# Layer 0's attention: scores once with queries on partitions, exp per half of the keys, turned by TensorE, against scores computed twice

## The chip, the core and the metric

The kernel runs on one core of one Trainium2 chip. The metric is device time of one execution in microseconds (us), the median over runs. A core has five engines that work at the same time and hand work to each other with semaphores: TensorE (PE; the loading of its stationary operand is listed apart, as PEld), VectorE (DVE), ScalarE (ACT), GpSimd (POOL) and SyncE (SP, which issues transfers). Each engine executes its own queue in order.

## The reference, cut to what matters

Two pre-norm transformer layers over `x` of 2 x 1024 x 128, in float32. Layer 0's attention has 8 heads; per head the queries and keys are 128 + 32 wide and come from a 32-wide latent:

```
scores = einsum('bhsd,bhtd->bhst', q, k) / sqrt(160)
attn   = softmax(scores, axis=-1)
o      = einsum('bhst,bhtd->bhsd', attn, v_c)
x      = x + concat(o) @ W_O + b_O
```

After it come a mixture of experts (8 experts, 2 per token, and a shared one), layer 1's causal attention (16 heads of 8) and layer 1's expert layer. The change touches layer 0's attention alone.

## The kernel before, in words

Products of weights are folded ahead, so that a head's score is a product over 64 numbers (32 latent and 32 rotary ones): `q2` holds two heads, one on partitions 0 to 63 and one on 64 to 127, and `key2` holds the keys twice. Two score matmuls of one pair of heads therefore sit on different row groups of the array. A batch and four heads make a unit `i` of 0 to 3; a unit is two pairs of heads (`pr`).

**Scores are computed twice.** `maxima0` (L562) computes them with queries on partitions: per 128 queries, 512 keys and pair of heads two matmuls into a two-bank PSUM tile `sc` (L574), and VectorE takes the negated maximum along the keys (L578). Every four query tiles the maxima are combined (L590), rounded by GpSimd into three bfloat16 parts (L593 to L601), and turned into rows by 16 small matmuls (`rows`, L603) that ScalarE copies out (L614). `attend0` (L618) computes the scores again with keys on partitions (L640), adds the negated maximum of each query with a bfloat16 matmul against ones (L646), and one ScalarE exp handles 128 keys x 2 heads x 512 queries (L651). The exps then already have the keys on partitions, so four column-tiled matmuls of 32 columns (`values`, L676) multiply them by the values, summed over the 8 key tiles in the PSUM tile `ud`. The denominators come from sums of the exps over key tiles (GpSimd, in the last unit VectorE, L662), closed by matmuls with ones (L693). `end` (L686) queues the rest: reciprocals of 128 x 128 tiles on VectorE (L706), the product (L709), a projection by `w_vo` (L714) and an add to `x` (L718).

PSUM has 8 banks: `ps` three tiles of two banks, `pn` and `pu` one each.

**What sets the order.** Instructions are issued in the order in which the program makes them on PE, DVE, POOL and SP (`IN_ORDER`, L44); ScalarE's are placed by the scheduler. The passes are generators that advance in turns (L831): one step of `maxima0`, one of `attend0` that starts `LAG` = 23 steps later (L736), one of `more`, which brings queries of the next unit (L544) and the preparation of batch 1 (L491). In the last steps (L838) the routing of batch 0 (`route`, L224) and the gathers of its rows (`get`, L386) are put beside. What is left of `late` runs among the first expert blocks (`quotients`, L988). All these end with unit 3; the expert blocks (L891) follow on PE.

Of the kernel before, what the change touches and what calls it, by code (L numbers as in the profile page):

```python
# [29 lines left out]
DA = DC + 1  # L30
QSCALE = 1.0 / math.sqrt(128 + DR)
# [20 lines left out]
def two_layers(ctx: ExitStack, tc: tile.TileContext, a: dict, out: bass.AP):  # L52
# [166 lines left out]
    w_vo = u_pool.tile([P, 2, D], F32, name="w_vo", bufs=1)  # L219
# [181 lines left out]
    with ExitStack() as att:  # L401

        ps = att.enter_context(tc.tile_pool(name="ps", bufs=3, space=PSUM))
# [5 lines left out]
        e0_pool = att.enter_context(tc.tile_pool(name="e0", bufs=10))  # L409
        s_pool = att.enter_context(tc.tile_pool(name="s", bufs=4))  # L410

        def bank0():
            return ps.tile([P, 512], F32, tag="ps", name="bank0")

        def spare0():
            t = e0_pool.tile([P, 2, 512], F32, tag="ex0", name="spare")
            return t.rearrange("p a b -> p (a b)")

        quot_bank = [lambda: pn.tile([P, 512], F32, tag="pn", name="y")]
# [3 lines left out]
        w_lat = load("w_lat", [P, 160], a["w_lat"])  # L423
        b_q = load("b_q", [DC, 1], a["b_q"])
# [5 lines left out]

        g = wa.tile([DA, H0, DC + DR], F32, name="g")
        nc.scalar.dma_start(g[:, :, DC : DC + DR], a["w_qr"])
# [22 lines left out]
        ctx_b, qs, last_rows = {}, {}, {}  # L455

        def products():
            gp = ps.tile([P, H0, DA], F32, tag="ps", name="gp")
            for h in range(H0):
                nc.tensor.matmul(  # L460
                    gp[:DA, h, :], w_up[:, 0, h, :], w_up[:, 1, h, :], start=True, stop=True
                )
            nc.vector.tensor_copy(g[:, :, 0:DC], gp[:DA, :, 0:DC])
            nc.vector.tensor_scalar(gc, gp[:DA, :, DC], QSCALE, None, ALU.mult)

        def output():


            vo = ps.tile([P, 2, D], F32, tag="ps", name="vo")
            for hg in range(2):  # L470
                for j in range(4):
                    h = 4 * hg + j
                    nc.tensor.matmul(
                        vo[DC * j : DC * (j + 1), hg, :], w_up[:, 2, h, 0:DC], w_o[:, h, :],
                        start=True, stop=True,
                    )
# [14 lines left out]
        def prepare(b):  # L491

            xt = xt_pool.tile([P, S], F32, name="xt")
            xn = e0_pool.tile([P, NT, D], F32, tag="ex0", name="xn0")
            yield from layernorm_steps(b, bank0, xt, xn, fine=b > 0, pool=b > 0, wait=4, by=nc.gpsimd if b else nc.vector)
            cq = lat.tile([DA, S], F32, name="cq")
            nc.gpsimd.memset(cq[DC:DA, :], 1.0)
# [3 lines left out]
            pk = ps.tile([P, S], F32, tag="ps", name="pk")  # L501
            for i in range(2):
                cols = slice(512 * i, 512 * (i + 1))
                nc.tensor.matmul(
                    pq[:DC, cols], w_lat[:, 0:DC], xt[:, cols], start=True, stop=True
                )
            for i in range(2):
# [4 lines left out]
            nc.vector.tensor_scalar(cq[0:DC, :], pq[:DC, :], b_q, None, ALU.add)  # L512
# [6 lines left out]
            pv = ps.tile([P, NT, DC], F32, tag="ps", name="pv")  # L519
# [9 lines left out]
            pc = ps.tile([P, NT, H0], F32, tag="ps", name="pc")  # L529
            for n in range(NT):  # L530
                nc.tensor.matmul(
                    pc[:, n, :], cq[:, n * P : (n + 1) * P], gc, start=True, stop=True
                )
            nc.vector.tensor_copy(cc.rearrange("p h n -> p n h"), pc)
            yield
# [8 lines left out]
        def queries(i):  # L544

            b, hg = divmod(i, 2)
            cq = ctx_b[b][0]
            qs[i] = []
            for pr in range(2):
                pq = ps.tile([P, S], F32, tag="ps", name="pq")  # L550
                h = 4 * hg + 2 * pr
                for c in range(2):
                    cols = slice(512 * c, 512 * (c + 1))
                    nc.tensor.matmul(  # L554
                        pq[:, cols], g[:, h : h + 2, :], cq[:, cols], start=True, stop=True
                    )
                q2 = q_pool.tile([P, S], F32, tag="q2", name="q2")
                nc.scalar.activation(q2, pq, AF.Copy, scale=QSCALE)
                qs[i].append(q2)
                yield  # L560

        def maxima0(i):  # L562

            b, hg = divmod(i, 2)
            _, key2, _, cc = ctx_b[b]
            mx2 = small.tile([P, 4, NT, 2], F32, name="mx2a", bufs=2)
            rows = None
            for st in range(NT):
                for c in range(2):
                    for pr in range(2):  # L570
                        sc = ps.tile([P, 2, 512], F32, tag="ps", name="sc")
                        for j in range(2):
                            r = slice(64 * j, 64 * (j + 1))
                            nc.tensor.matmul(  # L574
                                sc[:, j, :], qs[i][pr][r, st * P : (st + 1) * P],
                                key2[r, 512 * c : 512 * (c + 1)], start=True, stop=True,
                            )
                        nc.vector.tensor_reduce(  # L578
                            mx2[:, 2 * pr : 2 * pr + 2, st, c], sc, AX.X, ALU.max,
                            negate=True,  # L580
                        )
                        yield
                    if rows and c:
                        rows()
                        rows = None
                if st % 4 == 3:
                    half = st // 4
                    sts = slice(4 * half, 4 * half + 4)
                    m4 = small.tile([P, 4, 4], F32, name="m4", bufs=2)
                    nc.vector.tensor_reduce(m4, mx2[:, :, sts, :], AX.X, ALU.min)  # L590

                    ch = cc[:, 4 * hg : 4 * hg + 4, sts]
                    nc.gpsimd.tensor_tensor(m4, m4, ch, ALU.subtract)  # L593
                    nc.gpsimd.tensor_tensor(m4, m4, ch, ALU.add)
                    mp = mps[half]
                    for k in range(3):
                        nc.gpsimd.tensor_copy(mp[:, :, :, k], m4)
                        if k < 2:
                            r = small.tile([P, 4, 4], F32, name=f"mq{k}", bufs=2)
                            nc.gpsimd.tensor_tensor(r, m4, mp[:, :, :, k], ALU.subtract)  # L600
                            m4 = r  # L601

                    def rows(half=half, mp=mp):  # L603
                        pm = ps.tile([P, 2, 512], F32, tag="ps", name="pm")
                        for j in range(4):
                            for n in range(4):
# [8 lines left out]

            last_rows[i] = rows

        def attend0(i):  # L618


            b, hg = divmod(i, 2)
# [938 lines left out]
```

## Time and profile before

| | |
|---|---|
| median of 9 runs | 946.29 us (940.41 to 952.91) |
| profiled execution | 948.51 us, of which the span is 946.8 us |
| first score matmul (L574) | 22.0 us from the span's start |
| last values matmul (L676) of layer 0 ends | about 421 us |
| first expert block's turned rows (L902) | 424.1 us |
| PE, DVE, ACT, POOL busy over the span | 92%, 60%, 44%, 44% |
| mean granted TensorE clock | 0.971 |

Times below are microseconds from the span's start. In groups, a line is: source line, engine, operation, output <- input, shapes, count, busy time and mean duration. In timelines it is: start, length from the first start to the last end of merged instructions, engine, line, operation, count, and in brackets the idle time before and what ended it. A float32 matmul is recorded as two instructions, a float32 transpose (a matmul against the identity) as one. PE records overlap, since matmuls are pipelined; the time a matmul takes of the queue is read from start to start, and when its result is ready from its end.

### The profile page before, as it was taken

The page shows a single profiled execution, that of the slowest core. Times are in us where ns is not written, and L with a number is a line of the kernel's source. Part 1 is how long each engine was busy: PE and PEld are TensorE (multiplying, and loading weights), DVE is VectorE, ACT ScalarE, POOL GpSimd, SP SyncE. Part 2 cuts the span into 40 slices and gives each one's busy share as a digit, 9 for nine tenths or more (in the row PEclk, how much of TensorE's full clock was granted, in tenths as well). Part 3 has the DMA queues.
Part 4 walks back from the last instruction along what each step waited for, and adds up shares of the span by engine and source line. Part 5 has one row for each costly group of instructions (what it writes and reads, how often), then busy time and mean ns, then how long its engine had stood idle before and what let it go on. Part 6 is the DMA issues. An engine that isn't in the chain of part 4 may idle for free.

```text
span 946.8 us, 14370 instructions
## 1 busy us (share of the span) xinstructions
PE 867.1 (92%) x5308; PEld 426.9 (45%) x5308; DVE 572.1 (60%) x999; ACT 416.9 (44%) x685; POOL 413.4 (44%) x572
## 2 busy tenths in 40 slices
PE   5899999999999999999899789888889999889986
PEld 2543334443333333437675457553334444544334
DVE  4765553536464569756632484776787767666613
ACT  1024433443334343454322144245467665666672
POOL 3018794756584941356046320018432432313521
PEclk9799999999999999999989999988899999999999
DMA  9100000000000000013212126014233123020000
GB/s 284 32 1 1 1 1 1 1 1 1 1 1 2 1 17 7 9 28 103 31 52 45 19 64 144 31 42 71 33 70 70 37 41 52 2 63 15 19 1 23
DMA packets 32825, 33.48 MB, mean 35 GB/s; under 512 B 5548, under 2 KB 30028, under 8 KB 31596
## 3 DMA queue, kind: packets, MB, share of 16 engines
q1 hardware_dynamic: 26882, 25.02, 11.3%
q0 software_dynamic: 4544, 5.91, 3.6%
q10 hardware_dynamic: 1331, 1.65, 0.5%
q8 instruction: 43, 0.70, 0.3%
q14 instruction: 25, 0.20, 0.1%
HBM read 24.10 MB, written 8.45 MB: 34 GB/s over the span
## 4 chain that ended last, share of the span: by engine, by line
PE 70%; DVE 14%; ACT 4%; issue 4%; DMA 4%; POOL 3%; SPq 0%; POOLq 0%; ACTq 0%; DVEq 0%
PE sc L574 12%; PE sc L640 11%; PE ud L676 6%; PE up L1298 6%; PE banks L1155 4%; DVE mx L1165 4%; PE gub L917 4%; PE bank L1273 4%; ACT ex L1278 3%; PE sc L646 3%; DVE mx2a L578 2%; PE yblk L945 2%; PE gu L871 2%; PE den L693 1%; PE pq L554 1%
## 5 line engine op out<-in xcount | busy, mean ns | idle before, releaser
L578 DVE TENSOR_REDUCE mx2a<-sc 128x2 f32<-128x1024 f32 x128 | 154.6, 1217 | 131.8 <-PE sc L574 131.7
L651 ACT ACTIVATE ex<-sc 128x1024 f32<-128x1024 f32 x128 | 131.1, 1024 | 196.9 <-PE sc L646 192.3
L1165 DVE TENSOR_REDUCE mx<-banks 128x2 f32<-128x1024 f32 (+3 forms) x160 | 174.6, 1113 | 65.3 <-PE banks L1160 54.9
L1278 ACT ACTIVATE ex<-bank 128x512 f32<-128x512 f32 (+2 forms) x320 | 157.8, 558 | 101.0 <-PE bank L1273 97.5
L574 PE MATMUL sc<-key,q 64*128 64x512 f32 x512 | 148.6, 633 | 1.7 <-DVE mx2a L578 1.7
L662 POOL TENSOR_TENSOR sum<-sum,ex 128x1024 f32<-128x1024 f32 x60 | 139.7, 2353 | 8.8 <-ACT ex L651 8.7
L640 PE MATMUL sc<-q,key 64*128 64x512 f32 x512 | 140.6, 602 | 0.4 <-DVE probs L242 0.4
L1282 POOL TENSOR_SCALAR_AFFINE_SELECT ex<-ex 128x128 f32<-128x128 f32 (+1 forms) x192 | 66.8, 371 | 133.7 <-ACT ex L1278 129.9
L1155 PE MATMUL banks<-kp,qp 72*128 72x512 bf16 (+3 forms) x384 | 100.8, 335 | 6.0 <-DVE mx L1165 4.2
L1273 PE MATMUL bank<-qp,kp 75*128 75x512 bf16 (+3 forms) x384 | 96.2, 333 | 9.1 <-ACT ex L1278 6.1
L393 POOL DMA_INDIRECT xb<-xn,row x46 | 53.1, 1154 | 93.6 <-PE bank L902 35.3
L1298 PE MATMUL up<-ex,vp 128*32 128x512 f32 (+3 forms) x768 | 80.3, 514 | 3.6 <-POOL ex L1282 3.6
L574 PEld LDWEIGHTS sc<-key,q 64*128 64x128 f32 x512 | 49.3, 189 | 64.7 <-issue 51.2
L640 PEld LDWEIGHTS sc<-q,key 64*128 64x128 f32 x512 | 51.1, 188 | 60.6 <-issue 43.3
L978 POOL DMA_INDIRECT got<-ys,pos x32 | 41.3, 1291 | 77.3 <-DMA ys<-yb 64.0
L917 PE MATMUL gub<-wall,xbt 128*128 x184 | 65.1, 478 | 8.3 <-DVE mx L1165 6.2
L676 PE MATMUL ud<-ex,val 128*32 128x512 f32 x512 | 68.3, 604 | 0.0
L1155 PEld LDWEIGHTS <-qp 72*128 72x128 bf16 x384 | 37.8, 100 | 50.6 <-issue 34.2
L662 POOL TENSOR_TENSOR sum<-ex,ex 128x1024 f32<-128x1024 f32 x12 | 28.0, 2354 | 71.4 <-ACT ex L651 71.4
L922 ACT ACTIVATE slb<-gub 128x352 f32<-128x352 f32 x46 | 21.4, 464 | 77.1 <-PE gub L917 77.0
L923 DVE TENSOR_TENSOR hds<-slb,gub 128x352 f32<-128x352 f32 x46 | 23.7, 515 | 50.2 <-ACT slb L922 50.2
L646 PE MATMUL sc<-mr,onesb 64*128 64x512 bf16 x256 | 53.2, 378 | 0.0
(267 smaller groups left out, 1084.3 us busy)
## 6 DMA issues: line engine op xcount, KB each, us to landing
qp<-parts SPq DMA_DIRECT2D x72, 64.0 KB
kp<-parts SPq DMA_DIRECT2D x72, 64.0 KB
parts<-qk SPq DMA_DIRECT2D x24, 128.0 KB
ys<-yb SPq DMA_DIRECT2D x10, 256.0 KB
wall<-in_ffn_gate_dram SPq DMA_DIRECT2D x1, 1584.0 KB
wall<-in_ffn_up_dram SPq DMA_DIRECT2D x1, 1584.0 KB
wall<-in_ffn_down_dram SPq DMA_DIRECT2D x2, 576.0 KB
x<-in_h_dram SPq DMA_DIRECT2D x4, 256.0 KB
```

What stands on the lines that cost most here:

```text
L574: nc.tensor.matmul(sc[:, j, :], qs[i][pr][r, st * P : (st + 1) * P], key2[r, 512 * c : 512 * (c + 1)], start=True, stop=True,)
L578: nc.vector.tensor_reduce(mx2[:, 2 * pr : 2 * pr + 2, st, c], sc, AX.X, ALU.max, negate=True,)
L640: nc.tensor.matmul(sc[:, j, :], key2[r, k * P : (k + 1) * P], qs[i][pr][r, cols], start=True, stop=False,)
L651: nc.scalar.activation(ex, sc, AF.Exp)
L662: adder.tensor_tensor(t, a1, ex, ALU.add)
L676: nc.tensor.matmul(ud[DC * j : DC * (j + 1), :], val[:, k, :], es[j // 2][:, j % 2, :], start=(k == 0), stop=(k == NT - 1),)
L917: nc.tensor.matmul(gu[:, s, 0:FF], xbts[j // 4][:, (j % 4) * P : (j % 4 + 1) * P], flat[:, bass.ds(e0 + FF * s, FF)], start=True, stop=True,)
L1155: nc.tensor.matmul(sc[:, n, 0:w], qp[0:KP, j, s0 : s0 + P], kp[0:KP, j, c0:c1], start=True, stop=not diag,)
L1165: nc.vector.tensor_reduce(to, sc[:, :, 0:w], AX.X, ALU.max, negate=True)
L1273: nc.tensor.matmul(sc[:, j, 0:w], kp[0 : KP + 3, j0 + j, t0 : t0 + P], qp[0 : KP + 3, j0 + j, lo:hi], start=True, stop=True,)
L1278: nc.scalar.activation(ex[:, :, 0:w], sc[:, :, 0:w], AF.Exp, scale=SCALE1)
L1298: nc.tensor.matmul(up[WH * j : WH * (j + 1), lo - c0 :], vps[b][:, k, h : h + WH], es[j], start=(k == 0), stop=end,)
```

## The change

Layer 0's scores are computed once, with queries on partitions. A block is 256 queries (`QT` = 2 tiles) of one pair of heads, 32 blocks in all; per block four tiles of 128 queries x 512 keys x 2 heads (`scores`). VectorE takes the negated maximum over this half of the keys, two small VectorE operations pass it through a rounding by `cc`, and ScalarE applies exp per head with the maximum as per-partition bias and the sum as accumulated output (`accum_out`). TensorE then turns the exps in 128 x 128 pieces (`weights`, four steps `k` of two banks with four transposes each); the banks are copied to SBUF by ScalarE, every fourth copy by VectorE (`evict`). `values` multiplies them by the values, with the two halves of the keys of each head on partition groups of their own, in `uds`. At a block's end small tensors give the factor of each half, exp(common minimum - own) / denominator (`scale_a` to `scale_c`); it is widened by GpSimd to 128 columns, turned by TensorE and copied by ScalarE (`scale_d`), multiplied in (`times`) and projected (`add`; `w_vo` holds each head's product twice).

PSUM is now: `ps` two tiles of two banks (scores), `pt` two banks (`turned`, shared by the exps' transposes, `scale_d` and the projection's result), `pn` and `pu` one each. ScalarE's order is the program's too (`ALL_IN_ORDER`). Steps of `weights` run four steps behind `scores`. The latent queries are kept on two row groups (`CQ`), so that the two halves of a query matmul run on different rows; `queries` makes one pair of heads per four blocks. The routing of batch 0 and its gathers are put beside batch 1's blocks. The work removed is: the second scores, the bfloat16 matmuls, the rows, the sums on GpSimd, the denominators' matmuls, and the wide reciprocals.

The diff, cut to its core:

```diff
-        ps = att.enter_context(tc.tile_pool(name="ps", bufs=3, space=PSUM))
+        ps = att.enter_context(tc.tile_pool(name="ps", bufs=2, space=PSUM))
+        pt = att.enter_context(tc.tile_pool(name="pt", bufs=2, space=PSUM))
...
+        def turned():
+            return pt.tile([P, 512], F32, tag="pt", name="turned")
+
+        quot_bank = [turned]
...
+        def scores(n):
+            b, pr, c = BLOCKS[n]
...
+            for t in range(QT):
+                st = QT * c + t
+                for m in range(2):
+                    flush0()
+                    sc = ps.tile([P, 2, 512], F32, tag="ps", name="sc")
+                    for j in range(2):
+                        r = slice(64 * j, 64 * (j + 1))
+                        nc.tensor.matmul(
+                            sc[:, j, :], q2[r, st * P : (st + 1) * P],
+                            key2[r, 512 * m : 512 * (m + 1)], start=True, stop=True,
+                        )
+                    lo = low[:, t, m, :]
+                    nc.vector.tensor_reduce(lo, sc, AX.X, ALU.max, negate=True)
+                    ch = cc[:, 2 * pr : 2 * pr + 2, st]
+                    nc.vector.tensor_tensor(lo, lo, ch, ALU.subtract)
+                    nc.vector.tensor_tensor(lo, lo, ch, ALU.add)
+                    ex = e0_pool.tile([P, 2, 512], F32, name="ex0")
+                    exps[n][2][t, m] = ex
+                    def last(t=t, m=m, sc=sc, ex=ex):
+                        for j in range(2):
+                            nc.scalar.activation(
+                                ex[:, j, :], sc[:, j, :], AF.Exp, bias=low[:, t, m, j : j + 1],
+                                accum_out=tot[:, t, m, j : j + 1],
+                            )
+                    due0.append(last)
+                    yield
...
+        def evict(to, src):
+            copies[0] += 1
+            if copies[0] % 4:
+                nc.scalar.copy(to, src)
+            else:
+                nc.vector.tensor_copy(to, src)
+
+        def weights(n):
...
+            def scale_a():
+                both = small0("both", True)
+                nc.vector.tensor_tensor(both, low[:, :, 0, :], low[:, :, 1, :], ALU.min)
+                by = small0("by")
+                nc.vector.tensor_tensor(
+                    by, both.unsqueeze(2).to_broadcast(shape), low, ALU.subtract
+                )
+                nc.scalar.activation(by, by, AF.Exp)
+                by_block["by"] = by
+            def scale_b():
...
+                nc.gpsimd.tensor_tensor(tot, tot, by, ALU.mult)
+                den = small0("den", True)
+                nc.gpsimd.tensor_tensor(den, tot[:, :, 0, :], tot[:, :, 1, :], ALU.add)
+            def scale_c():
...
+                nc.vector.reciprocal(den, den)
+                nc.gpsimd.tensor_tensor(
+                    by, by, den.unsqueeze(2).to_broadcast(shape), ALU.mult
+                )
+                wide = u_pool.tile([P, QT, 4, DC], F32, name="wide")
+                nc.gpsimd.tensor_copy(
+                    wide,
+                    by.rearrange("p t m j -> p t (m j)").unsqueeze(3).to_broadcast([P, QT, 4, DC]),
+                )
+            def scale_d():
+                tp = turned()
+                for t in range(QT):
+                    nc.tensor.transpose(
+                        tp[:, t * P : (t + 1) * P],
+                        by_block["wide"][:, t].rearrange("p k r -> p (k r)"), ident,
+                    )
+                by_t = u_pool.tile([P, W], F32, name="by_t")
+                nc.scalar.copy(by_t, tp[:, 0:W])
...
+            def times():
+                ot = u_pool.tile([P, W], F32, name="ot0")
+                nc.vector.tensor_tensor(ot, ud, by_block["t"], ALU.mult)
...
+            def add():
+                y = quot_bank[0]()[:, 0:W].rearrange("p (n d) -> p n d", d=D)
+                for t in range(QT):
                     nc.tensor.matmul(
+                        y[:, t, :], by_block["ot"][:, t * P : (t + 1) * P], w_vo[:, pr, :],
+                        start=True, stop=True,
                     )
+                n0 = b * NT + QT * c
+                nc.vector.tensor_add(x[:, n0 : n0 + QT, :], y, x[:, n0 : n0 + QT, :])
+
+            mine = [scale_a, scale_b, scale_c, scale_d, times, add]
+            for k in range(4):
                 if late:
                     late.pop(0)()
+                if ended and k < 3:
+                    ended.pop(0)()
+                es = []
+                for m in range(2):
+                    tp = turned()
+                    for j in range(2):
+                        for t in range(QT):
+                            i = QT * j + t
+                            nc.tensor.transpose(
+                                tp[:, i * P : (i + 1) * P],
+                                ex[t, m][:, j, k * P : (k + 1) * P], ident,
+                            )
+                    e = et_pool.tile([P, 2, W], F32, name="et")
+                    evict(e.rearrange("p j w -> p (j w)"), tp)
+                    es.append(e)
+                def values(k=k, es=es):
+                    for m in range(2):
                         for j in range(2):
+                            r = 64 * m + DC * j
                             nc.tensor.matmul(
+                                ud[r : r + DC, :], val[:, 4 * m + k, :], es[m][:, j, :],
+                                start=(k == 0), stop=(k == 3),
                             )
+                late.append(values)
+                if k:
+                    mine.pop(0)()
+                yield
+            ended.extend(mine)
...
         passes = zip_longest(
-            chain(*map(maxima0, range(n))), after(LAG, chain(*map(attend0, range(n)))), more()
+            chain(*map(scores, range(n)), once(flush0)),
+            after(2 * QT, chain(*map(weights, range(n)))),
+            more(),
         )
-        with tc.manual_schedule(engines=IN_ORDER):
-            for _ in islice(passes, (n - 1) * UNIT + LAG - 2):
+        with tc.manual_schedule(engines=ALL_IN_ORDER):
+            for _ in islice(passes, QT * n + 2 * QT + 4):
                 pass
-            ahead = chain(hurry(route(0, bank0, spare0), 2), get(0))
+            ahead = chain(hurry(spread(route(0, bank0, spare0), 2), 3), get(0))
             for _ in passes:
                 next(ahead, None)
```

## The prediction, on record before the result

> **What bounds the kernel now.** I read the page's busy shares first, then its costliest groups, then a table of stages, then a timeline of PE. Layer 0's attention takes 22 to 421 us, 399 of the span's 946.8 us. In the table of stages (columns: time, then busy time of PE, PEld, DVE, ACT and POOL, then the granted clock) PE is busy almost without a gap where both passes run, and no other engine is above 65%:
>
> ```profile
> 22.00:65.00 43.00, 39.14 (x188) 21.44 (x186) 28.90 (x30) 3.06 (x3) 3.90 (x8) 0.84 0.15 28
> 65.00:370.00 305.00, 304.10 (x1774) 119.83 (x1772) 168.19 (x198) 122.93 (x126) 199.09 (x142) 1.00 0.01 3
> 370.00:421.00 51.00, 49.70 (x321) 19.45 (x319) 39.93 (x73) 26.37 (x27) 24.06 (x22) 0.97 0.06 16
> ```
>
> Busy is no proof of a peak, so I take starts from the PE timeline (start, length):
>
> ```profile
> 215.76 1.02 PE L574 MATMUL sc<-key,q 64*128 64x512 f32 x4
> 216.62 1.02 PE L640 MATMUL sc<-q,key 64*128 64x512 f32 x4
> 217.47 0.38 PE L646 MATMUL sc<-mr,onesb 64*128 64x512 bf16 x2
> ...
> 219.72 1.06 PE L676 MATMUL ud<-ex,val 128*32 128x512 f32 x8
> 220.72 1.13 PE L574 MATMUL sc<-key,q 64*128 64x512 f32 x4
> ```
>
> A score pair holds PE for 0.86 us (215.76 to 216.62), 0.96 after another form of matmul; the ones 0.22 or 0.31 (219.41 to 219.72); four values matmuls 1.00. So PE's queue is the bound, and the stage is worth what its queue holds, until another engine or a wait is later.
>
> **PE's work, old and new.** Old: 128 score pairs x 0.96 = 123; 128 second pairs with their ones x 1.1 = 141; 64 values x 1.0 = 64; denominators 8 x 1.75 = 14; projections 8 x 1.1 = 9; rows 8 x 0.6 = 5; 8 query tiles x 1.75 = 14; batch 0's leftovers (folded weights, value and bias products between 24 and 50 us) 12, batch 1's preparation 10, routing 8. Sum 400 against 399 seen: nothing is left to waits.
>
> New: 128 score pairs stay (123). 1024 transposes come in. Their price stands in the expert blocks:
>
> ```profile
> 452.75 0.47 PEld L902 LDWEIGHTS bank<-ident,xb 128*128 128x128 f32 x4
> 452.86 0.60 PE L902 MATMUL bank<-ident,xb 128*128 128x128 f32 x4
> 453.19 0.89 PEld L917 LDWEIGHTS gub<-wall,xbt 128*128 128x128 f32 x4
> ```
>
> Four take from 452.75 to 453.19: 0.11 us each, though one record lasts 0.27. With 0.1 for the change of form, eight cost 0.98 per score pair: 125. Values have the same columns in matmuls of 256: half of 1.0 per pair, plus up to 0.1: 68 to 80. The factors' two transposes 0.22 and the projection's two matmuls 0.55, for 32 blocks: 25. Query tiles with both halves on different rows: 8 x 0.96 = 8. Leftovers 14 (output products doubled), preparation 10, routing 8. Sum 381 to 393. So the change, which removes two fifths of PE's list, puts nearly as much back: **6 to 19 us less, I take 13.** PE's work alone is 2.47 us per score tile and 10.7 per block (4 x 2.47 + 0.22 + 0.55).
>
> At this place the Trainium skill speaks against the change. "TensorE: Matmul & The Clock Gate", section "Part 4: PE-mode transpose", gives about 275 ns for a transpose in a kernel and says that transposes do not count as PE activity for the clock. The record's 0.27 us agrees with the former as a latency, but the spacing is 0.11; by 275 ns each the sum would be 169 us larger, and by half the clock during transposes 113 us. The stage 440 to 460 us, which holds such transposes, has a granted clock of 1.00, so I follow the rows.
>
> **The other engines.** Exps: 256 of 128 x 512 with a per-partition bias. Rows for that shape:
>
> ```profile
> L1435 ACT ACTIVATE h<-bank,e x8: 679/688/689, 821.1 to 940.1; 128x512 f32<-128x512 f32 x8
> ...
> L123 ACT COPY xt<-bank x12: 579/586/599, 13.7 to 691.8; 128x512 f32<-128x512 f32 x12
> ```
>
> A biased activation takes 0.69 against 0.60 for L876 without, and a second one directly behind starts 0.1 before the first ends (two of L1278 span 1.09). The accumulated sum is in no row. It costs between nothing and a whole small activation (L244, 128 x 64: 0.26); I take 0.09, like the bias, its nearest operand: 0.78 each, 0.69 in a row. ACT per tile: 1.38 + 1.5 copies x 0.55 + 0.2 (per block a 256-column copy of 0.38 and a small exp of 0.2, per four blocks a query copy of 1.02) = 2.4. DVE per tile: maximum 1.23 (L578), two small operations at 0.20 to 0.21 (L131 to L141 stand 0.20 apart), half a 512-column copy from PSUM (128 columns take 0.28 at L1325 and 256 take 0.41 at L477, so 512 take 0.68), 0.36 of block work (two small operations and a reciprocal at 0.2, two 256-column products at 0.41, over four): 2.3. POOL loses 140 us of sums and has little left. So three engines stand at 2.3 to 2.7 us per tile, each in order, and **what decides is the waits between them.**
>
> **The waits, followed through one block.** In the built order the third step of a block puts both halves' transposes through the same bank: the projection's result holds the other. The first step does the same with the factors' bank. Hand-over between engines is 0.05 (L574 ends 210.01, L578 starts 210.05). Zero is the start of the scores of step 3; T0, T1 are a step's two banks.
>
> - Step 3: scores ready 1.13, maximum 1.17 to 2.40, corrections to 2.80; T1 is queued to 2.48, ready 2.65. DVE copies T1's bank 2.80 to 3.50, reciprocal (0.20, L248) to 3.72; POOL multiplies (0.20, L150) and widens. A POOL conversion takes 0.24 for 64 and 0.29 for 128 columns (L817), so 0.40 for 256; L1379's two-operand add, 0.46 for 128, would make it 0.78. I take 0.40: ready 4.45.
> - Step 0: PE did its scores and, once DVE's copy was there, its values by 4.0, then waits; factors 4.5 to 4.72; T0 to 5.16; ACT copies the factors 4.95 to 5.33 (0.38 for 256 columns, by L123's slope); only then T1, to 5.84. Steps 3 and 0 take 5.84 where PE's work is 5.2.
> - Step 1: scores start at 5.84, so the maximum runs 7.01 to 8.24, corrections to 8.64, product 0.41 to 9.09, copy of T1 to 9.77, two small operations to 10.2, ACT's small exp to 10.45. Behind it on ACT, in order, wait the two exps of step 1's scores, to 11.9, and behind those step 2's copy of T0, to 12.42.
> - Step 2: T1 shares T0's bank, so it starts at 12.47 and ends at 12.91. Its scores and projection were done by 10.7; PE waited 1.3.
>
> A block takes **12.9 us, where PE's work is 10.7.** Behind PE in these waits stand the next scores, hence DVE's next maximum: nothing covers them. Over 31 blocks with both passes: 2.2 x 31 = 68.
>
> **The rest.** Queries take one of only two score tiles, so that the next scores wait for an exp pair of the tile just made: about 1.4 x 7 = 10. The four tiles ahead of the first weights, and the four steps after the last scores, lack a partner: 5. Routing's and preparation's small DVE work is counted as hidden in DVE's gaps; without them it is about 12 more. Gathers moved ahead on POOL are hidden (PE waited 3 us at most between 421 and 424, and fewer leftovers follow): 0. Start: more operands to load, one query tile less ahead: 0.
>
> Sum: -13 + 68 + 10 + 5 = +70 on 948.5, thus 1018.5 for a profiled execution; the median of the runs lies 2.2 lower: **1016 us.**
>
> **Rivals.**
> - *The waits are covered* (faster): if the shared bank, and the exps queued ahead of its copy, held nobody up, the stage would be PE's list: 946.3 - 13 = 933, at best 927. For: ACT and DVE each have less than 2.5 us per tile. Against: the chain through steps 1 and 2 is made of measured durations and adds to 7.07 against 5.5 of PE. It decides if less than 0.4 us per block is left of 2.2. If half of it and of the 15 for queries, lead and tail is left: 1016 - 34 - 7 = 975.
> - *The exps' and widening's price* (slower): sums at 0.26 lengthen the pair twice in step 2's chain, 0.34 x 31 = 11; widening at 0.78 adds 0.38 x 31 = 12; routing and preparation not hidden 12: 1051.
> - *The clock*: it fell to 0.84 in 22 to 65 us, where PE had waits. At 0.9, PE's 10.7 grows by 1.2, of which half lies on the chain: 0.6 x 31 = 19: 1035, with the former 1070.
> - *It doesn't do what it says*: the built order has 256 score matmuls instead of 512 in source, so that is excluded.
>
> **Numbers.** Forecast (985 to 1040) 0.60; slower prices or clock (1040 to 1075) 0.18; half the waits (955 to 985) 0.11; the same within 0.5%, which is about what a measurement of this kernel can tell from no change, 0.03; covered waits, faster, 0.08. The range of 972 to 1056 leaves out two in ten. Faster 0.08, same 0.03, slower 0.89.
>
> **What would show it.** Right: score tiles in a pattern of two steps near 2.5 us and two longer ones (about 3.4 and 4.6), PE idle before the transposes with ACT's copies as releaser, blocks near 12.9 us, last values near 490 us, POOL nearly idle, later stages unchanged. Wrong: blocks near 10.7; transposes 0.2 or more apart; exps above 0.9; or a granted clock under 0.9 in this stage.

## The result, and the profile after

The kernel after takes 1005.49 us (median of 20 runs, 1001.96 to 1013.1) against 947.14 (62 runs of the kernel before, 939.45 to 959.88): ratio 1.0627, 95% interval 1.0606 to 1.0648. The forecast of 1016 (972 to 1056) holds it. The profiled execution took 1007.53 us, its span 1005.8 us, 59.0 more than before. Expert blocks begin at 481.64 us instead of 424.15, so 57.5 of the 59.0 lie ahead of that point, 3.5 of them before the first scores, and 1.5 behind it.

The page's busy times, and three of its costliest groups, of the changed stage:

```profile
PE 895.7 (89%) x5980; PEld 484.9 (48%) x5980; DVE 627.2 (62%) x1404; ACT 576.0 (57%) x1307; POOL 245.2 (24%) x562
...
L608 ACT ACTIVATE ex<-sc,low 128x512 f32<-128x512 f32 x256 | 173.7, 686 | 13.4 <-DVE low L602 9.0
L714 PE MATMUL turned<-ident,ex 128*128 128x128 f32 x1024 | 151.3, 281 | 22.8 <-ACT et L629 21.9
L629 ACT COPY et<-turned 128x512 f32<-128x512 f32 x192 | 112.4, 586 | 72.7 <-PE turned L714 65.8
```

PE is still by far the busiest engine. The last column of the transposes' group (L714), the idle time ahead of them and what ended it, is new: 21.9 us in which PE waited for ScalarE's copies. The table of stages has the columns of the one shown of before:

```profile
22.00:60.00 38.00, 32.49 (x192) 17.48 (x191) 19.90 (x43) 17.84 (x44) 3.30 (x5) 0.78 0.15 31
60.00:105.00 45.00, 41.61 (x302) 21.16 (x302) 32.38 (x84) 32.85 (x84) 6.17 (x20) 1.00 0.00 1
105.00:170.00 65.00, 60.49 (x418) 31.52 (x416) 38.53 (x83) 42.02 (x105) 12.59 (x25) 0.97 0.00 1
170.00:245.00 75.00, 68.94 (x493) 34.00 (x492) 47.16 (x109) 54.76 (x137) 5.62 (x22) 1.00 0.00 1
245.00:310.00 65.00, 59.34 (x423) 29.98 (x418) 43.82 (x112) 48.88 (x120) 7.76 (x26) 1.00 0.03 9
```

The granted clock is not what was lost: it is 0.78 at the start, where before had 0.84 in 22 to 65 us, and 0.97 to 1.00 in the other rows; over the whole of layer 0's attention it is 0.98 in both kernels (22 to 424 and 25.5 to 481.6 us). PE now has gaps of 6 us in 75, where before it had 0.9 in 305 (65 to 370 us). GpSimd is nearly idle. A block repeats every 12.62 to 12.63 us, read from one start of the widening copy (L668) to the next. PE's timeline of one block, steps 3, 0, 1 and 2:

```profile
262.50 1.13 PE L593 MATMUL sc<-key,q 64*128 64x512 f32 x4
263.56 0.64 PE L726 MATMUL uds<-et,val 128*32 128x256 f32 x8
264.13 1.09 PE L714 MATMUL turned<-ident,ex 128*128 128x128 f32 x8
265.15 1.13 PE L593 MATMUL sc<-key,q 64*128 64x512 f32 x4
266.21 0.64 PE L726 MATMUL uds<-et,val 128*32 128x256 f32 x8
266.83 0.44 PE L677 MATMUL turned<-ident,wide 128*128 128x128 f32 x2
267.10 1.28 PE L714 MATMUL turned<-ident,ex 128*128 128x128 f32 x8
268.31 1.13 PE L593 MATMUL sc<-key,q 64*128 64x512 f32 x4
...
272.66 0.71 PE L695 MATMUL turned<-w_vo,ot 128*128 128x128 f32 x4
273.21 0.60 PE L714 MATMUL turned<-ident,ex 128*128 128x128 f32 x4
274.54 0.66 PE L714 MATMUL turned<-ident,ex 128*128 128x128 f32 x4 [0.73 <-ACT et L629]
275.12 0.70 PE L593 MATMUL sc<-key,q 64*128 64x512 f32 x2
```

From scores to scores the steps take 2.65 (262.50 to 265.15), 3.16, 2.66 (268.31 to 270.97) and 4.15 us: the pattern of the forecast, 2.5, 3.4, 2.5 and 4.6. In the last one PE stands between 273.6 and 274.54 for a copy. But the two steps with no wait at all are longer than the 2.47 of the forecast. ScalarE in step 2 of the same block:

```profile
272.46 0.67 ACT L608 ACTIVATE ex<-sc,low 128x512 f32<-128x512 f32 x1
273.03 0.19 ACT L608 ACTIVATION_READ_ACCUMULATOR ex<-sc,low 128x1 f32 x1
273.13 0.68 ACT L608 ACTIVATE ex<-sc,low 128x512 f32<-128x512 f32 x1
273.70 0.20 ACT L608 ACTIVATION_READ_ACCUMULATOR ex<-sc,low 128x1 f32 x1
273.90 0.59 ACT L629 COPY et<-turned 128x512 f32<-128x512 f32 x1
```

The accumulated sum is a record of its own, 0.2 us long, of which most lies under the exp. Both exps were over at 273.90, and the copy started then. The bank's last transpose was issued at about 273.53 and is ready 0.27 later, at 273.81: the copy was at most 0.09 late.

The theory taken to the runs: (a) the shared bank holds PE up, about 1 us per block, without help from ScalarE's queue; (b) PE's own list is no shorter than before, because of something in each step that the forecast had too small. The rivals: ScalarE's queue (exps, sums, the small exp), GpSimd's widened factors, the query tiles, or dearer transposes.

### The profile page after: what moved, and what is told of

It is laid out like the page before. It is cut to its first block, busy times and chain, and to the rows that moved or that the text cites. A ratio compares the mean times of both kernels' runs of the same rounds, so it can differ in the third digit from the quotient of the medians.

```text
span 1005.8 us, 16902 instructions
## 1 busy us (share of the span) xinstructions
PE 895.7 (89%) x5980; PEld 484.9 (48%) x5980; DVE 627.2 (62%) x1404; ACT 576.0 (57%) x1307; POOL 245.2 (24%) x562
## 4 chain that ended last, share of the span: by engine, by line
PE 60%; DVE 20%; ACT 11%; issue 4%; POOL 3%; DMA 1%; ACTq 0%; POOLq 0%; DVEq 0%
PE sc L593 10%; PE turned L714 8%; PE up L1297 6%; PE gub L916 5%; PE banks L1154 5%; DVE mx L1164 4%; DVE low L598 4%; PE bank L1272 4%; ACT ex L608 4%; PE uds L726 4%; ACT ex L1277 2%; PE yblk L944 2%; ACT et L629 2%; DVE et L631 2%; PE gu L870 2%
## 5 line engine op out<-in xcount | busy, mean ns | idle before, releaser
L598 DVE TENSOR_REDUCE low<-sc 128x2 f32<-128x1024 f32 x128 | 156.3, 1221 | 123.2 <-PE sc L593 123.0
L608 ACT ACTIVATE ex<-sc,low 128x512 f32<-128x512 f32 x256 | 173.7, 686 | 13.4 <-DVE low L602 9.0
L714 PE MATMUL turned<-ident,ex 128*128 128x128 f32 x1024 | 151.3, 281 | 22.8 <-ACT et L629 21.9
L629 ACT COPY et<-turned 128x512 f32<-128x512 f32 x192 | 112.4, 586 | 72.7 <-PE turned L714 65.8
L714 PEld LDWEIGHTS turned<-ident,ex 128*128 128x128 f32 x1024 | 112.6, 142 | 66.8 <-ACT et L629 29.0
L726 PE MATMUL uds<-et,val 128*32 128x256 f32 x1024 | 87.9, 395 | 1.1 <-ACT et L629 0.9
L726 PEld LDWEIGHTS uds<-et,val 128*32 128x32 f32 x1024 | 22.9, 108 | 99.6 <-ACT et L629 63.2
L395 POOL DMA_INDIRECT xb<-xn,row x46 | 48.1, 1046 | 76.7 <-issue 38.6
L656 POOL TENSOR_TENSOR tot<-tot,by 128x8 f32<-128x8 f32 x32 | 6.5, 204 | 224.1 <-ACT by L651 224.1
L593 PEld LDWEIGHTS sc<-key,q 64*128 64x128 f32 x512 | 40.5, 191 | 38.9 <-issue 19.1
```

The source lines that it names most:

```text
L593: nc.tensor.matmul(sc[:, j, :], q2[r, st * P : (st + 1) * P], key2[r, 512 * m : 512 * (m + 1)], start=True, stop=True,)
L598: nc.vector.tensor_reduce(lo, sc, AX.X, ALU.max, negate=True)
L608: nc.scalar.activation(ex[:, j, :], sc[:, j, :], AF.Exp, bias=low[:, t, m, j : j + 1], accum_out=tot[:, t, m, j : j + 1],)
L629: nc.scalar.copy(to, src)
L714: nc.tensor.transpose(tp[:, i * P : (i + 1) * P], ex[t, m][:, j, k * P : (k + 1) * P], ident,)
L726: nc.tensor.matmul(ud[r : r + DC, :], val[:, 4 * m + k, :], es[m][:, j, :], start=(k == 0), stop=(k == 3),)
```

## The experiments

The kernel before was timed beside each; ratios are to it. Where a line number in a profile differs by a few from that of the kernel after, the edit moved it.

**A third bank** for the turned tiles (the single bank `pn` goes into the pool):

```diff
-        pt = att.enter_context(tc.tile_pool(name="pt", bufs=2, space=PSUM))
-        pn = att.enter_context(tc.tile_pool(name="pn", bufs=1, space=PSUM))
+        pt = att.enter_context(tc.tile_pool(name="pt", bufs=3, space=PSUM))
...
-            return pn.tile([P, 512], F32, tag="pn", name="bank0")
+            return pt.tile([P, 512], F32, tag="pt", name="bank0")
```

> The transposes get a third PSUM bank (the preparation's own bank is given up and its small tiles take turns with them), so the second group of step 2 no longer has to wait for the first group's copy. My theory (the shared bank itself holds PE): step 2 falls from 4.16 to about 3.2 us, the step with the factors from 3.16 to about 3.0, a block from 12.63 to about 11.5, the whole by about 35 us, to some 970. Rival one (ScalarE's queue is what is late, a bank only moves the wait to the values matmuls): 0 to 10 us less. Rival two (all steps are bound by PE's list): no change.

Measured: 976.99 us (972.96 to 978.45), ratio 1.028 (1.0203 to 1.0358); blocks 11.42 to 11.43 us. PE's timeline of the step with the projection:

```profile
237.17 1.13 PE L592 MATMUL sc<-key,q 64*128 64x512 f32 x4
238.23 0.70 PE L725 MATMUL uds<-et,val 128*32 128x256 f32 x8
238.86 0.71 PE L694 MATMUL turned<-w_vo,ot 128*128 128x128 f32 x4
239.41 1.04 PE L713 MATMUL turned<-ident,ex 128*128 128x128 f32 x8
240.38 1.13 PE L592 MATMUL sc<-key,q 64*128 64x512 f32 x4
```

All eight transposes follow each other; the step takes 3.21 instead of 4.15, and the step with the factors 2.91 instead of 3.16. A steady block fell by 1.2 us and the whole by 28.5 (30.0 between the two profiled spans): (a) holds. Half of the loss is still there.

**The small exp behind the exps** (it moves from `scale_a` to the start of `scale_b`):

```diff
-                nc.scalar.activation(by, by, AF.Exp)
                 by_block["by"] = by
...
                 by = by_block["by"]
+                nc.scalar.activation(by, by, AF.Exp)
```

> The small exp of the block's factors is issued after step 2's copies instead of ahead of the exps of step 1's scores. The blind prediction's chain (small exp, exp pair, copy, second transposes) would give back about 1 us per block, 30 us. The trace of the changed kernel speaks against it: the copy starts 0.09 us after its transposes are ready, so the exps ahead of it are done in time; by that reading 0 to 5 us less.

Measured: 1003.93 us (1003.11 to 1008.12), ratio 1.059 (1.0511 to 1.0669), which can't be told from the changed kernel's. The small exp's place in ScalarE's queue ahead of the copy is not the cause.

**The factors one step later** (`scale_d`, `times` and `add` in steps 1 to 3 instead of 0 to 2):

```diff
-                if ended and k < 3:
+                if ended and k > 0:
```

> The factors' transposes, the product and the projection come one step later each (steps 1, 2, 3 instead of 0, 1, 2), so that GpSimd's widening has a step more before PE needs it. If the wait for GpSimd (0.5 us in the step with the factors) is what lengthens that step: 0.5 us per block, 15 us less. If VectorE's chain from maximum to maximum sets the length of that step: no change.

Measured: 1007.12 us (1005.13 to 1009.87), ratio 1.0614 (1.0536 to 1.0693), blocks 12.56 to 12.58. The wait for GpSimd went and nothing was gained: it was only 0.05 us, and the factors' copy (`by_t`, L682), which shares its bank with a half's transposes, holds PE in the new place as in the old.

**Queries in banks of their own** (each half in the single bank `pn`, copied by itself, instead of one of the two score tiles):

```diff
-            pq = ps.tile([P, S], F32, tag="ps", name="pq")
...
+                pq = bank0()
...
+                nc.scalar.activation(q2[:, cols], pq, AF.Copy, scale=QSCALE)
+                yield
```

> Queries are made in two halves through the one-bank pool, in two steps, and no longer take one of the two score tiles. Blocks with queries now last 14.9 instead of 12.63 us, seven times. If the wait for a score tile and for ScalarE's copy is the reason: about 1.3 of the 2.25 us go, 9 us in all; if it is PE's own work on the queries: 0 to 2 us.

Measured: 1008.45 us (1001.32 to 1011.0), ratio 1.0609 (1.052 to 1.0699). Blocks with queries and nothing else beside them fell from about 14.9 to 14.3 us, which would be 0.6 x 7 = 4; those beside preparation or routing, which use the same bank, moved by -2.9 to +2.4, and all blocks together by -2.75. The time can't be told from the changed kernel's, so that the queries' whole price stays open here.

**Each transpose of the exps issued twice:**

```diff
+                            for _ in range(2):
                                 nc.tensor.transpose(
```

> Each of the 1024 transposes of the exps is issued twice into the same place, and nothing else is changed. Theory (PE's queue is the bound in all four steps of a block, and a transpose takes 0.107 us of it, as the spacing in the timeline says): eight more per step, 0.86 us, block from 12.63 to about 16.0 us, 32 blocks: +105 to +112 us, about 1110 to 1118. Rival A (a transpose really costs the 0.27 us that its record lasts): +200 us or more, or a granted clock under 0.9 in the stage. Rival B (the clean steps have slack on PE and another engine paces them): less than +60 us, and clean steps under 3.2 us.

Measured: 1085.52 us (1084.05 to 1095.23), ratio 1.1485 (1.1411 to 1.1558), 80 us more than the changed kernel; blocks 15.04, granted clock over the span 0.975. Neither the theory's 105 nor a rival's figure. The timeline shows why:

```profile
230.29 1.13 PE L593 MATMUL sc<-key,q 64*128 64x512 f32 x4
...
231.92 0.71 PE L695 MATMUL turned<-w_vo,ot 128*128 128x128 f32 x4
232.47 2.10 PE L715 MATMUL turned<-ident,ex 128*128 128x128 f32 x16
234.50 1.13 PE L593 MATMUL sc<-key,q 64*128 64x512 f32 x4
...
236.12 1.97 PE L715 MATMUL turned<-ident,ex 128*128 128x128 f32 x16
238.02 1.13 PE L593 MATMUL sc<-key,q 64*128 64x512 f32 x4
```

A step without waits grew from 2.65 to 3.52 (234.50 to 238.02): 0.87 for eight more, **0.109 us each**, close to the 0.107 of the theory. The step with the projection grew by 0.06 only: in this build the second half's tile was given the projection's bank, which VectorE's add had freed, and no longer the first half's. A row of the loading of its operand shows this (L700 is the add):

```profile
233.47 0.86 PEld L715 LDWEIGHTS turned<-ident,ex 128*128 128x128 f32 x8 [0.21 <-DVE x L700]
```

So the wait for the copy, 0.9 us per block, was gone. The step with the factors grew by 0.63, since the copy of the factors was now covered. 0.87 + 0.87 + 0.63 + 0.06 is the 2.4 us by which a block grew.

**No accumulated sums** (the denominators are a constant, so that this part of the computation is left out):

```diff
+            nc.gpsimd.memset(tot, 512.0)
...
-                                accum_out=tot[:, t, m, j : j + 1],
```

> The accumulated sums of the 256 exps are left out (the denominators are then a constant, so this part of the computation is changed). Theory (ScalarE's exps are not late in any step, PE and the shared bank are): each pair of exps gets 0.1 to 0.2 us shorter and the time moves by 0 to 4 us, block 12.5 to 12.63. Rival (the exps and what waits behind them on ScalarE set steps 1 and 2, as the prediction's chain had it): two pairs per block earlier by 0.2 to 0.4 us, thus 0.2 to 0.4 x 31 = 6 to 12 us less.

Measured: 1006.04 us (1003.33 to 1008.73), ratio 1.0614 (1.0563 to 1.0666); blocks 12.62 to 12.63. Two exps in a row, merged into one line of ScalarE's timeline:

```profile
237.25 1.27 ACT L609 ACTIVATE ex<-sc,low 128x512 f32<-128x512 f32 x2
```

One of them takes 0.687, so the second starts 0.58 behind the first, against 0.67 with sums (272.46 to 273.13). The sum costs ScalarE's queue 0.09 us each, and the kernel nothing that can be told: a steady block is as long as with them, so the exps are not what is late here.

**Third bank, and the factors one step later:** both edits above.

> The third bank for turned tiles (as in the first experiment) and the factors' step moved one step later (as in the third) at once. Theory (with the shared bank gone, what is left above PE's list is the wait for GpSimd's widened factors, about 0.5 us per block): block from 11.43 to 10.9 to 11.2 us, 977 minus 7 to 17, thus 960 to 970 us. Rival (as in the third experiment alone: the wait only moves to another place, here the copies of the turned tiles): 974 to 979 us, block 11.4. In neither case below the 947 of the kernel before, since PE's list is 4 x 2.65 + 0.72 = 11.3 as read from the clean steps.

Measured: 969.37 us (965.44 to 970.71), ratio 1.0213 (1.0164 to 1.0262); blocks 11.36 to 11.37. The time lies in the theory's range, the block does not: a steady block gained 0.06 only, so with three banks the factors' wait was nearly gone already; of the 5.4 us that the blocks gained together, 3.5 lie in four of them beside the routing.

**All waits eased:** besides, the small exp later, and queries in halves in banks of the turned tiles.

> Third bank, factors one step later, the small exp behind the exps, and queries made in two halves in a bank of the turned tiles instead of one of the two score tiles. Theory (PE's list is not shorter than before's: 11.3 us per block, so all waits taken away give at best about the time before): 950 to 968 us, blocks without queries 10.9 to 11.3 us, blocks with queries about 1 us longer. Rival (the prediction's sum of PE's list, 10.7 per block and 13 us less than before in all, holds, and only waits are between): 933 to 945 us, blocks at 10.7.

Measured: 964.47 us (963.46 to 970.15), ratio 1.017 (1.0127 to 1.0213); blocks 11.32. PE's timeline has steps of 2.66, 2.87 (with the factors), 2.65 and 3.14 us (with the projection), each score group, values and transposes directly behind the other:

```profile
239.71 1.13 PE L592 MATMUL sc<-key,q 64*128 64x512 f32 x4
240.77 0.64 PE L725 MATMUL uds<-et,val 128*32 128x256 f32 x8
241.34 1.09 PE L713 MATMUL turned<-ident,ex 128*128 128x128 f32 x8
242.37 1.13 PE L592 MATMUL sc<-key,q 64*128 64x512 f32 x4
...
245.24 1.13 PE L592 MATMUL sc<-key,q 64*128 64x512 f32 x4
...
247.89 1.13 PE L592 MATMUL sc<-key,q 64*128 64x512 f32 x4
...
251.03 1.13 PE L592 MATMUL sc<-key,q 64*128 64x512 f32 x4
```

So 11.32 is PE's list itself. With the waits of its steady blocks taken away the change still does not reach the time before: (b) holds, and the forecast's 10.7 per block is ruled out. Blocks with queries and nothing else beside them take up to 13.03, 1.7 more than a steady one, where about 1 was expected.

**Values of two steps back to back,** on top of that:

```diff
-                if late:
+                while late and k % 2 == 0:
                     late.pop(0)()
```

> The eighth experiment's kernel with one edit: the values of two steps are issued back to back, every second step. Same instructions. Theory (what makes PE's list 2.65 us per step instead of the 0.86 + 0.50 + 0.86 = 2.22 of scores, values and transposes by themselves is the change of the form of matmul, three per step, 0.43 / 3 = 0.14 each): five changes instead of six per two steps, thus 0.14 x 2 x 31 = 9 us less than the eighth's 964, about 955, blocks at 11.0. Rival (the 0.43 is in the matmuls themselves, not in the change): 962 to 966, blocks at 11.3.

Measured: 954.18 us (950.98 to 958.26), ratio 1.0103 (1.0049 to 1.0157); blocks 11.04 to 11.05.

```profile
250.18 1.13 PE L592 MATMUL sc<-key,q 64*128 64x512 f32 x4
251.24 1.07 PE L725 MATMUL uds<-et,val 128*32 128x256 f32 x16
252.24 1.09 PE L713 MATMUL turned<-ident,ex 128*128 128x128 f32 x8
253.26 1.13 PE L592 MATMUL sc<-key,q 64*128 64x512 f32 x4
```

The same instructions, two changes of form (scores of 64 rows, values of 32 columns, full transposes) fewer per block, 0.28 us less: 0.14 per change. Sixteen values take 1.00 where two groups of eight took 0.57 each. Eight more thus cost 0.43, and not the 0.50 of the theory, so that scores, values and transposes by themselves make 0.86 + 0.43 + 0.86 = 2.15. The three changes of a step of 2.65 then cost about 0.50: 0.20 at the end of the scores, 0.14 of the values and 0.16 of the transposes. The 0.14 that the theory had as the mean of the three is the price of the one kind that this edit takes away. This is the fastest version found; it is still 1% slower than the kernel before.

**Two steps at once** (two score tiles, values of two steps, sixteen transposes; each head's exp a step of its own in ScalarE's order):

```diff
+        def two(steps):
+            for i, _ in enumerate(steps):
+                if i % 2:
+                    yield
...
+                    if k % 2 == 0:
+                        flush0(3 if m else 1)
                     evict(e.rearrange("p j w -> p (j w)"), tp)
```

> The eighth experiment's kernel with two steps taken together: two score tiles, then the values of two steps, then sixteen transposes; ScalarE's exps put between the copies so that its order does not hold up the banks. Same work. Theory (0.14 us per change of form): three changes instead of six per two steps, 0.43 x 2 = 0.86 us less per block, blocks at about 10.5, 964 - 0.86 x 31 = about 937, thus faster than the kernel before (948). Rival A (ScalarE with 2.5 and VectorE with 2.35 us per step cannot keep up with PE at 2.6 in a fixed order): PE waits for copies or exps, blocks at 11 or more, 955 or more. Rival B (changes of form cost nothing): blocks at 11.3, 964.

Measured: 1082.73 us (1078.9 to 1089.56), ratio 1.1479 (1.1411 to 1.1547); rival A, and worse than it said; a steady block takes 13.34. PE waits for exps (both score tiles are needed at once) and for copies that stand behind three exps:

```profile
247.47 1.13 PE L594 MATMUL sc<-key,q 64*128 64x512 f32 x4
248.81 1.13 PE L594 MATMUL sc<-key,q 64*128 64x512 f32 x4 [0.21 <-ACT ex L608]
...
255.24 0.66 PE L716 MATMUL turned<-ident,ex 128*128 128x128 f32 x4 [1.83 <-ACT et L630]
```

The clock is a second loss: over 22 to 550 us the granted clock is 0.91, where the ninth experiment had 1.00 over 22 to 430. The scores of two tiles, eight records, took 3.63 us at 240.84, where the granted clock was 0.53, and 1.99 at 255.83, where it was 1.00. The 2.0 us by which a steady block is longer than the eighth experiment's make 63 of the 118 us; the rest is not taken apart.

**As this, the corrections on GpSimd** (the two small operations behind the maximum):

```diff
-                    nc.vector.tensor_tensor(lo, lo, ch, ALU.subtract)
-                    nc.vector.tensor_tensor(lo, lo, ch, ALU.add)
+                    nc.gpsimd.tensor_tensor(lo, lo, ch, ALU.subtract)
+                    nc.gpsimd.tensor_tensor(lo, lo, ch, ALU.add)
```

> As the tenth, with the two small operations behind each maximum on GpSimd instead of VectorE (VectorE 0.4 us less per score tile, GpSimd 0.4 more). If VectorE is what is late in the tenth: 5 to 15 us less than the tenth. If PE's queue is (theory): within 3 us of it. If ScalarE is: the same, or a few us more, since each exp starts later by the two hand-overs, about 0.1 us.

Measured: 1098.19 us (1094.64 to 1100.06), ratio 1.1615 (1.1562 to 1.1667), 15 us more than the tenth: taking this load off VectorE did not help. That the longer way from maximum to exp is the cause was not tested by itself; the granted clock was 0.90 over 22 to 550 us.

**Scores apart, transposes of two steps together** (score tile, values of two steps, score tile, sixteen transposes):

```diff
-                for m in range(2):
+                for m in range(4 if k % 2 else 0):
...
+                    flush0((1, 1, 2, 0)[m])
```

> The ninth experiment's kernel with the transposes of two steps put together as well, between two score tiles that stay apart: score tile, values of two steps, score tile, sixteen transposes. Values run up to three steps behind; the factors' and the projection's matmuls stand behind the values; ScalarE's four exps stand between the copies (first head, copy, second head, copy, next tile's two heads, copy). Same work. Theory (0.14 us per change of form, and PE the bound): four changes instead of five per two steps, blocks at 10.75 instead of 11.04, 954 - 9 = 945, thus about as the kernel before (within 0.5%). Rival (ScalarE's and VectorE's order holds up PE as in the tenth, where two score tiles followed each other): blocks above 11.2, more than 958.

Measured, on another chip, where the kernel before took 964.04: 989.52 us (982.32 to 994.58), ratio 1.0271 (1.0223 to 1.0319); blocks 11.41. The rival's outcome, for two reasons that the timeline shows:

```profile
246.22 1.13 PE L594 MATMUL sc<-key,q 64*128 64x512 f32 x4
247.31 1.07 PE L730 MATMUL uds<-et,val 128*32 128x256 f32 x16
248.31 0.71 PE L696 MATMUL turned<-w_vo,ot 128*128 128x128 f32 x4
248.95 1.13 PE L594 MATMUL sc<-key,q 64*128 64x512 f32 x4
250.01 2.04 PE L717 MATMUL turned<-ident,ex 128*128 128x128 f32 x16
252.07 1.13 PE L594 MATMUL sc<-key,q 64*128 64x512 f32 x4
```

The projection (L696), which stood ahead of transposes before, now has scores behind it: it takes 0.64 instead of 0.55, so a change of form had come back and the count was five again; the factors' transposes, in the next pair of steps, take 0.37 instead of 0.27 (254.13 to 254.50). And the transposes hold 2.06, where 16 x 0.109 and a change make about 1.9: the next scores wait 0.2 for the second head's exp, which was put behind a copy.

## Why the prediction came out right, and which of its terms did not

The sum was +70 and the span moved by +59. Two large terms were off, in opposite directions.

- **PE's list, forecast 6 to 19 us shorter: wrong in size and sign.** A step was put at 2.47 us; it holds PE for 2.65 (the eighth experiment's blocks, 11.32, against the forecast's 10.7). Over 32 blocks that is 20 us, and against the 347 that the forecast's score pairs, transposes, values (at the middle of their range), factors and projections add to it is 362 - 347 = 15. So the list is about 2 us longer than before's, not 13 shorter. The term that was mis-sized is the change of form of matmul: 0.1 for scores and for transposes, up to 0.1 for values. The scores hold PE for 1.06 instead of 0.96, values 0.57 instead of 0.53, transposes 1.02 instead of 0.98. Against the 2.15 of the three by themselves the changes cost 0.50. The ninth experiment takes two away and gains 0.28 per block. What in a change of form takes the time no run shows. A slip in the sum was smaller: half of 1.0 plus up to 0.1 is 64 to 77 over 128 pairs, not 68 to 80.
- **The transposes' 0.11: right,** 0.109 when doubled. The Trainium skill, "TensorE: Matmul & The Clock Gate", section "Part 4: PE-mode transpose", has about 275 ns for a bfloat16 one in a kernel and says that transposes do not count as PE-busy the same way, so that the full clock does not engage. Here 0.27 is the record's length, not its price, and the granted clock was 1.00 in three of the stages above, and in every stage of 60 to 484 us with the transposes doubled (fifth experiment). The measurement decides, for transposes among other matmuls; no stage holds them alone.
- **The waits, 2.2 us per block, 68 in all: right in place, too large.** Against the eighth experiment's steps, 0 and 2 wait 0.29 and 1.01 (3.16 - 2.87 and 4.15 - 3.14), together 1.3 x 31 = 41. Step 2's reason failed in its middle: the copy of T0 was to wait behind the exps, over at 11.9, and to end at 12.42. The exps were over at 11.40 (273.90, from 262.50), and the copy waited 0.09 at most. What held T1 up is the shared bank, which the third bank shows (28.5 us), while neither the small exp's place nor the sums moved the time. In step 0 the widened factors were late by 0.05, not by 0.45; the copy of the factors ahead of T1 (0.26) was right.
- **Sums 0.09, widening 0.40, VectorE's copy 0.68:** measured 0.09 (sixth experiment), 0.40 and 0.69. The bounds kept for dearer ones were not needed.
- **Queries, 1.4 x 7 = 10:** a block with queries is 2.25 longer, of which 1.06 is the matmuls' own time: 1.2 x 7 = 8.
- **Routing and preparation hidden: right.** The blocks exceed 12.63 by 34 us in all; less 7 x 2.25 for queries that leaves 18, what the forecast had for their matmuls in PE's list.
- **Start 0: open.** The first scores came at 25.5 us instead of 22.0, but at 23.2 to 24.5 in the profiles of the first four experiments and the sixth, and at 22.1 in the eighth's, so these 3.5 can't be put down to the change for certain.
- **Gathers 0: the bound was loose.** Of the 3 us "at most" PE waited for none: before, it ran the last values of layer 0 until 422.5, not about 421, and then the denominators' matmuls up to the expert blocks.

List +2, waits 41, queries 8, start 3.5 and later stages 1.5 make 56 against 59.0; 3 us are left for the lead and the tail, which the forecast had at 5 and no run took by themselves.

The rivals: *waits covered* fell by its own condition, since 1.3 us per block were left; the eighth experiment shows besides that covered waits would have given about 964, not 933; 15 of these 31 us are the list, the others are not taken apart. *Half the waits* described the waits better than the forecast (41 of 68 left), yet its time of 975 was missed, mainly because the list had been too short. The dearer exps and the clock did not come.

That the time was hit is thus partly luck: 15 us too little on the list, 27 too much on the waits.

## What to carry to other kernels

When work is replaced on a full engine, read the new list's price from a step in its new company: short groups of matmuls of different form cost 0.14 to 0.20 us per change here, and three of them per step, with the transposes, ate what the removed second scores had freed. Give every tile that a full engine fills a bank whose last reader is long done, counting the small tiles (factors, projections, queries) that take their turn in the same pool. Before easing a wait, double or remove the suspected cost alone: here ScalarE's sums and the order of its small exp cost nothing that could be told, while one more bank gave back 28 us.

## What the runs showed of the hardware

- A change of the form of matmul on PE (64-row scores, 32-column values, full transposes) costs 0.14 to 0.20 us each (0.50 for the three of a step of 2.65); putting the values of two steps together gave back 0.14 for each change that went.
- An exp with an accumulated sum leaves a second record of 0.20 us on ScalarE, but holds its queue only 0.09 us longer.
- 128 x 128 float32 transposes follow each other every 0.109 us. The granted clock was 1.00 in stages where they are over a third of PE's matmul records (1024 of some 2950), and from 60 to 484 us with twice as many of them.
- Which bank a tile of a pool gets can change with an unrelated edit: with doubled transposes the second half's tile moved from the copied bank to the projection's, and a wait of 0.9 us per block vanished.
